# A deformable-convolution block with routed experts: output transposes one tap later, row differences two taps after their block, expert pieces in the gaps between stages

## The chip, the cores and the metric

The kernel runs on one core of a Trainium2 chip. The metric is the device time of one execution in microseconds, lower is better. The engines are TensorE (PE), VectorE (DVE), ScalarE (ACT), GpSimd (POOL) and SyncE (SP); POOL issues the indirect DMAs (gathers), SP the plain ones. Each engine works through its own list of instructions in order, and waits where an instruction's inputs or buffers are not ready.

## The reference

The input is `x`, 4 images of 256 channels and 64 x 64 positions, float32. Cut to what is computed:

```python
x = x + conv_ref(ln_c(x))          # ln_c: layer norm over channels at each position
t = to_tokens(x)                   # [4, 4096, 256]
t = t + ffn_ref(ln_t(t))           # ln_t: layer norm over each token's 256 values
return from_tokens(t)

def conv_ref(x):                   # three layers in a row
    for wo, bo, w, b in params:
        x = relu(deform_layer(x, wo, bo, w, b))
    return x

def deform_layer(x, w_off, b_off, w, b):
    om = conv3x3(x, w_off) + b_off            # 27 values at each position
    off, mask = om[:18], sigmoid(om[18:])     # (dy, dx) of 9 taps, 9 masks
    sampled = bilinear(x, base + off) * mask  # 9 samples of 256 channels each
    return einsum('bikhw,oik->bohw', sampled, w) + b

def ffn_ref(x):                    # 8 experts, the two best of each token
    probs = softmax(x @ gate_w + gate_b)
    cw = the two largest probs of each token, 0 elsewhere
    return sum over e of cw[:, e] * (gelu(x @ W1[e] + b1[e]) @ W2[e] + b2[e])
```

## The kernel before

**Stages.** The convolution work is cut into 12 stages, one for each layer and image, in the order (layer, image) = (0,0), (1,0), (0,1), (2,0), (1,1), (0,2), (2,1), (1,2), (0,3), (2,2), (1,3), (2,3); they are called stages 0 to 11. The order lets a stage's output table be finished while another image's stage runs. Only after stages 0, 10 and 11 is that not so: stages 1 and 11 gather from the table that the stage just ahead of them has filled, and after stage 11 there is no other. There `settle` runs all that is left of the side work at once.

**Blocks and taps.** A stage has 8 blocks of 512 positions, a block has 9 taps (`main_block`), and a tap has 4 samples of 128 positions. For a sample (`samples`), POOL gathers 128 rows of 4 table values for each channel (`g`, L467, 512 KB), DVE makes two interpolations (L473 and L478), ACT scales by the mask (L481). `turn` transposes samples in pairs on PE (`tp`, L496), two pairs behind the newest, and ACT copies them to `sT` (L499). `finish` multiplies a tap's `sT` by the tap's weights into `acc` (L519), and after tap 8 ACT writes the rectified rows to a window (`win`, L541).

**Tables.** Once a window's rows are there, `rows_done` starts two side generators. `store_table` makes the differences of neighbouring rows on DVE (`dd`, L272), transposes rows and differences on PE (L286), copies on ACT (`hv`, L291) and stores to the next layer's table from SP (L294). `off_block` makes the offset convolution `po` (L322) and the plan of gathers and coefficients of the next layer. In layer 2 `tokens` adds `x`, transposes, normalises, computes the gate (`lg`, L605 to L627: logits on DVE, then Exp on ACT) and the softmax and its two best (`sm`, L631, on DVE). Stages 0, 3 and 6 also prepare the tables of the next image (`pre_block`).

**Side work.** A generator put aside yields between its steps; `step(k)`, called after each tap, runs as many steps as make the list end with the block, one at least where any is left. `aside(3, ...)` says that a generator has three steps.

**Experts.** When a group of tokens is routed (`enqueue`), `begin` puts its expert steps on `tiles`, three pieces each: fetch weights and tokens (`w` L766, `zt` L778 on POOL), transposes (`ftp` L801), first product (`ph` L816), activation (`hT` L826), second product (`py` L832), bias (`y` L850 on DVE). There are five groups, images 0, 1 and 2 and the halves of image 3; `pump`, called after each tap, takes a piece each time that the group's pace allows: paces 5, 5, 2, 1.5 and 0 taps for a step. `drain` takes pieces without taps, in the last `settle` and after the last sample.

**Combine.** After a group's experts `end` queues the sums: for each 128 tokens two fetches of expert rows (`gy`, L868, on POOL, into four buffers) and two sums on DVE (`ta`, L883), at 0.5 credit, two of them to a tap. After the second of a pair the code goes on to the pair's transposes on PE (`otp`, L893), a copy on ACT (`o`, L899) and the store of the output.

**Order.** A scheduler places instructions in each engine's list. `behind()` places what is in it after the newest sample's DVE instruction (`self.last`), `later()` after the newest gather (`self.gathered`). The transposes of the sums are in neither.

Of the kernel before, what the change touches and what calls it, by code (L numbers as in the profile page):

```python
# [14 lines left out]
P = 128  # L15
# [56 lines left out]
class Group:  # L72


    def __init__(self, b, n0, n1):
        self.b, self.n0, self.n1 = b, n0, n1
        self.nm = f"{b}_{n0}"
        self.M = (n1 - n0) * TPB

        self.NF = 2 * self.M * P // FT + E - 1  # L80


        self.half = (self.NF + 1) // 2
        self.zt, self.acc, self.gy, self.py = {}, [], [], None
        self.order = [s // 2 + s % 2 * self.half for s in range(self.NF)]


class Weave:
# [3 lines left out]
    def __init__(self, ctx, tc, ins, out):  # L92
        nc = self.nc = tc.nc
        self.tc = tc
        self.ins = ins
        self.x = ins["x"].rearrange("b (c p) h w -> b p c (h w)", p=P)
        self.out_v = out.rearrange("b (c p) h w -> b p c (h w)", p=P)
        self.B = self.x.shape[0]

        def pool(name, bufs, **kw):  # L100
            return ctx.enter_context(tc.tile_pool(name=name, bufs=bufs, **kw))

        self.cst = pool("cst", 1)
        self.dram = pool("dram", 1, space=bass.MemoryType.DRAM)
        self.wkp = pool("wkp", 1)
        self.plan = pool("plan", 22)
        self.win = pool("win", 3)
        self.wt = pool("wt", 2)
        self.small = pool("small", 1)
        self.big = pool("big", 2)  # L110
        self.ffn = pool("ffn", 2)
        self.rt = pool("rt", 1)
        self.rt2 = pool("rt2", 2)
        self.gyp = pool("gyp", 4)
        self.smT = pool("smT", 2)
        self.smp = pool("smp", 8)
        self.gat = pool("gat", GB)
        self.ps = pool("ps", 3, space=bass.MemoryType.PSUM)
        self.ps1 = pool("ps1", 1, space=bass.MemoryType.PSUM)
        self.queue = []  # L120
        self.credit = 0.0
        self.side, self.plans_side = [], []
        self.last, self.gathered = None, None
        self.tiles = []
        self.tile_credit = 0.0
        self.pend, self.pairs = None, []
# [125 lines left out]
    def rows_done(self, l, b, n, wins):  # L252

        nc = self.nc
        w = wins[n]
        if n > 0:
            nc.scalar.copy(w[:, :, 0, :], wins[n - 1][:, :, RPB, :])
            nc.scalar.copy(wins[n - 1][:, :, RPB + 1, :], w[:, :, 1, :])  # L258
        self.aside(3, self.store_table(l, b, n, w))
        if n > 0:  # L260
            self.aside(6, self.off_block(l, b, n - 1, wins[n - 1]), True)
        if n == NB - 1:
            self.aside(6, self.off_block(l, b, n, w), True)

    def store_table(self, l, b, n, w):

        nc = self.nc
        nm = f"{l}_{b}_{n}"
        v = self.table(l, b).rearrange("(r c) f -> r c f", c=TC)
        dd = self.big.tile([P, CC, BLK], F32, tag="a", name=f"dd_{nm}")  # L270
        with self.behind():
            nc.vector.tensor_tensor(  # L272
                dd.rearrange("p c (r w) -> p c r w", w=W),
                w[:, :, 1 : RPB + 1, :],
                w[:, :, 0:RPB, :],
                ALU.subtract,
            )
# [32 lines left out]
    def off_block(self, l, b, n, w):  # L310
# [47 lines left out]
        yield  # L358
        with self.behind():
            nc.vector.tensor_tensor(  # L360
# [34 lines left out]
    def pre_block(self, b, n, wins, spare):  # L395
# [19 lines left out]
        rest = normalise(nc, self.small, h, h, self.eps_c, nm)  # L415
        with self.behind():
            next(rest)
        yield
        with self.behind():
            next(rest, None)  # L420
# [64 lines left out]
    def turn(self):  # L485
# [8 lines left out]
        for u in range(2):  # L494
            for c in range(CC):
                nc.tensor.transpose(  # L496
                    tp[:, c, u * P : (u + 1) * P], ss[u][:, c * P : (c + 1) * P], self.ident
# [53 lines left out]
    def tokens(self, b, n, r):  # L551
# [9 lines left out]
        yield  # L561
        with self.behind():
            nc.vector.tensor_tensor(r, r, xc, ALU.add)
# [16 lines left out]
        rest = normalise(nc, self.small, tok, z, self.eps_t, nm)  # L580
        with self.behind():
            next(rest)
        yield
        with self.behind():
            next(rest, None)
# [31 lines left out]
        yield  # L617
        with self.behind():
            nc.vector.tensor_tensor(
# [9 lines left out]
        sm = small("sm", (P, TPB))  # L629
        with self.behind():  # L630
            nc.vector.tensor_reduce(sm, lg, AX.X, ALU.add)  # L631
# [154 lines left out]
    def expert(self, grp, step):  # L786
# [20 lines left out]
        if step + 1 < grp.NF:  # L807
            with self.later():
                self.fetch(grp, step + 1)
# [31 lines left out]
    def products(self, grp):  # L841
# [6 lines left out]
        y = self.ffn.tile([P, FU, C], F32, tag="y", name=f"y_{grp.nm}_{f}")  # L848
        with self.behind():
            nc.vector.tensor_tensor(  # L850
# [7 lines left out]
    def combine_load(self, grp, n, t0):  # L858
        a = self.ffn.tile([P, 2, C], F32, tag="c", name=f"ta_{grp.nm}_{n}_{t0}")
        self.nc.sync.dma_start(a, self.t_dram[grp.b][grp.n0 + n][:, t0 : t0 + 2, :])  # L860
        grp.acc.append(a)

    def combine_fetch(self, grp, m):

        for i in range(2):
            g = self.gyp.tile([P, C], F32, tag="gy", name=f"gy_{grp.nm}_{m}_{i}")
            with self.later():
                self.nc.gpsimd.indirect_dma_start(  # L868
# [7 lines left out]
    def combine(self, grp, m):  # L876
# [3 lines left out]
        acc = grp.acc[0]  # L880
        with self.behind():
            for i in range(2):
# [3 lines left out]
                )  # L886
        if t == 0:
            return
        grp.acc.pop(0)
        tp = self.ps.tile([P, CC, 2 * P], F32, tag="tp", name=f"otp_{nm}")  # L890
        for t in range(2):
            for c in range(CC):
                nc.tensor.transpose(  # L893
                    tp[:, c, t * P : (t + 1) * P],
                    acc[:, t, c * P : (c + 1) * P],
                    self.ident,
                )
        o = self.ffn.tile([P, CC, 2 * P], F32, tag="o", name=f"o_{nm}")
        nc.scalar.copy(o, tp)  # L899
        p0 = grp.n0 * BLK + (m - 1) * P  # L900
        nc.sync.dma_start(self.out_v[grp.b, :, :, p0 : p0 + 2 * P], o)
# [19 lines left out]
    def end(self, grp):  # L921
# [64 lines left out]
    def run(self):  # L986
# [25 lines left out]
        for i, (l, b) in enumerate(self.stages):  # L1012
# [60 lines left out]
```

## Time and profile before

| | us |
|---|---|
| three runs | 7209.39, 7211.4, 7215.62 |
| median | 7211.4 |
| the profiled execution's own time | 7205.3 |
| its span in the profile | 7203.2 |

| stage | 0 | 1 | 2 | 3 | 4 | 5 | 6 | 7 | 8 | 9 | 10 | 11 |
|---|---|---|---|---|---|---|---|---|---|---|---|---|
| us from its first sample to the next stage's | 539 | 451 | 455 | 469 | 521 | 526 | 538 | 595 | 530 | 537 | 770 | 690 |

171 us lie ahead of the first sample and 413 behind the last, where the rest of the experts and the last sums run. A plain block of stages 1 and 2 takes 56.9 us. The mean clock that TensorE was granted is 0.96 of full speed. Combines fall in stages 7, 10 and 11 and behind the last sample.

How to read the lines: a group's line has the line of code, engine, operation, output and input with shapes and count, then its busy microseconds and mean nanoseconds, then the microseconds that its engine was idle just before, and what ended that. A line of waits has engine, tile and line, what ended the wait, then microseconds in all, times, longest. In the order of time a line has start, duration, engine, line, operation, and in brackets the idle time ahead of it. Matmuls are pipelined and their ends are modelled, and in the trace some of their records can be missing.

### The profile page before, as it was taken

How to read it: one execution, taken by the hardware profiler on the slowest of the kernel's cores; microseconds unless marked ns; L12 is line 12 of the kernel's file. 1: busy time of each engine (PE TensorE's matmuls, PEld its weight loads, DVE VectorE, ACT ScalarE, POOL GpSimd, SP SyncE). 2: the span in 40 equal slices, each digit the busy share in tenths (PEclk: the TensorE clock that was granted, in tenths of full speed). 3: DMA queues.
4: the chain of work that ended last, by engine and by line, in shares of the span. 5: the costliest groups of instructions: out<-in, count | busy, mean ns of one | idle time of the engine just before them, and what ended most of it. 6: DMA issues, size and time to landing. Idle time of an engine off the chain costs nothing. (4 is left out here: it accounts for less than half of the span.)

```text
span 7203.2 us, 90914 instructions
## 1 busy us (share of the span) xinstructions
PE 6450.5 (90%) x27800; PEld 3707.4 (51%) x27800; DVE 4974.0 (69%) x10828; ACT 3621.4 (50%) x7699; POOL 4291.6 (60%) x4210
## 2 busy tenths in 40 slices
PE   6899898889999999999987999999988699977987
PEld 2444444444545555556653555555555466644675
DVE  4777777778998767768876867677777465667521
ACT  4565555556764545556653455455554354544422
POOL 0654666666666656666666666666665564666543
PEclk8999999999999999999998999999999899988998
DMA  4988999989998889889998999898897787878643
GB/s 130 355 320 299 367 354 361 358 341 374 383 377 326 327 329 335 329 332 354 350 333 277 337 336 338 320 348 319 316 343 245 233 290 258 299 275 297 237 142 112
DMA packets 754764, 2224.87 MB, mean 309 GB/s; under 512 B 105880, under 2 KB 208024, under 8 KB 748520
## 3 DMA queue, kind: packets, MB, share of 16 engines
q0 software_dynamic: 549072, 1941.73, 73.3%
q1 hardware_dynamic: 205208, 277.34, 11.3%
q8 instruction: 224, 3.67, 0.2%
q14 instruction: 260, 2.13, 0.1%
HBM read 2160.68 MB, written 197.44 MB: 327 GB/s over the span
## 5 line engine op out<-in xcount | busy, mean ns | idle before, releaser
L467 POOL DMA_INDIRECT g<-tab,idx x3456 | 3516.9, 1018 | 1862.7 <-DVE s L478 687.2
L519 PE MATMUL acc<-sT,wk 128*128 128x512 f32 x6912 | 3451.5, 613 | 156.2 <-ACT sT L499 148.8
L473 DVE SCALAR_TENSOR_TENSOR g<-g,cf 128x512 f32<-128x512 f32 x3456 | 2556.5, 742 | 609.1 <-DMA g<-tab,idx 605.5
L478 DVE SCALAR_TENSOR_TENSOR s<-g,cf 128x256 f32<-128x256 f32 x3456 | 1658.6, 483 | 568.5 <-PE tp L496 270.8
L481 ACT ACTIVATE s<-s,cf 128x256 f32<-128x256 f32 x3456 | 1649.0, 509 | 675.2 <-DVE s L478 653.5
L499 ACT COPY sT<-tp 128x512 f32<-128x512 f32 x1728 | 997.6, 586 | 1592.9 <-PE tp L496 1588.0
L519 PEld LDWEIGHTS acc<-sT,wk 128*128 128x128 f32 x6912 | 1186.3, 195 | 973.8 <-issue 675.9
L496 PEld LDWEIGHTS tp<-ident,s 128*128 128x128 f32 x6912 | 886.2, 145 | 1325.8 <-ACT s L481 675.3
L496 PE MATMUL tp<-ident,s 128*128 128x128 f32 x6912 | 1258.0, 285 | 210.7 <-ACT s L481 195.9
L816 PE MATMUL ph<-fzT,w 128*128 128x256 f32 x2608 | 660.3, 387 | 34.0 <-DMA w<-in_W,wrow 16.1
L832 PE MATMUL py<-w,hT 128*128 128x256 f32 x2608 | 641.1, 387 | 30.3 <-ACT hT L826 28.3
L816 PEld LDWEIGHTS ph<-fzT,w 128*128 128x128 f32 x2608 | 476.6, 193 | 156.9 <-issue 39.3
L832 PEld LDWEIGHTS py<-w,hT 128*128 128x128 f32 x2608 | 478.9, 191 | 149.5 <-ACT hT L826 58.9
L766 POOL DMA_INDIRECT w<-in_W,wrow x163 | 169.9, 1043 | 519.5 <-issue 105.4
L826 ACT ACTIVATE hT<-ph,w 128x256 f32<-128x256 f32 x652 | 283.4, 471 | 372.2 <-PE ph L816 289.9
L778 POOL DMA_INDIRECT zt<-z,tok x326 | 335.7, 1030 | 134.6 <-issue 91.0
L868 POOL DMA_INDIRECT gy<-ys,slots x256 | 267.8, 1046 | 226.6 <-DVE ta L883 121.9
L322 PE MATMUL po<-win,wo 128*32 128x504 f32 (+1 forms) x2304 | 359.3, 600 | 14.6 <-ACT win L258 12.4
L850 DVE TENSOR_TENSOR y<-py,w 128x512 f32<-128x512 f32 x163 | 111.5, 684 | 255.8 <-PE py L832 248.2
L893 PE MATMUL otp<-ident,ta 128*128 128x128 f32 x256 | 67.8, 365 | 214.0 <-issue 145.4
L291 ACT COPY hv<-tpv 128x512 f32<-128x512 f32 x384 | 209.1, 592 | 96.7 <-PE tpv L286 72.1
L272 DVE TENSOR_TENSOR dd<-win 128x1024 f32<-128x1024 f32 x64 | 78.1, 1221 | 202.7 <-ACT win L541 202.7
(152 smaller groups left out, 3724.2 us busy)
## 6 DMA issues: line engine op xcount, KB each, us to landing
tab<-hv SPq DMA_DIRECT2D x384, 256.0 KB, 7.1
g<-tab,idx POOLq DMA_INDIRECT x3456, 6.9
ys<-y SPq DMA_DIRECT2D x163, 256.0 KB, 3.3
wk<-in_conv_w SPq DMA_DIRECT2D x108, 256.0 KB, 7.4
xc_pre<-in_x SPq DMA_DIRECT2D x32, 512.0 KB, 11.6
xr_tok<-in_x SPq DMA_DIRECT2D x32, 512.0 KB, 8.0
t<-t_tok SPq DMA_DIRECT2D x32, 512.0 KB, 5.9
ta<-t SPq DMA_DIRECT2D x64, 256.0 KB, 3.6
```

The lines of the kernel that those rows point to most:

```text
L322: nc.tensor.matmul(po[g * Q : (g + 1) * Q, :].rearrange("q (r w) -> q r w", w=W)[:, :, x0:x1], lhsT=self.wo[l][:, 3 * ky + kx, c, :], rhs= ...
L467: self.gathered = nc.gpsimd.indirect_dma_start(out=g.rearrange("p x s f -> p (x s f)"), out_offset=None, in_=self.table(*self.stages[i]), ...
L473: nc.vector.scalar_tensor_tensor(g[:, :, 0, :], g[:, :, 1, :], cf[:, j, 0:1], g[:, :, 0, :], ALU.mult, ALU.add,)
L478: self.last = nc.vector.scalar_tensor_tensor(s, g[:, 1, 0, :], cf[:, j, 1:2], g[:, 0, 0, :], ALU.mult, ALU.add)
L481: nc.scalar.activation(s, s, AF.Copy, scale=cf[:, j, 2:3])
L496: nc.tensor.transpose(tp[:, c, u * P : (u + 1) * P], ss[u][:, c * P : (c + 1) * P], self.ident)
L499: nc.scalar.copy(self.sT[:, :, t0 * P : (t0 + 2) * P], tp)
L519: nc.tensor.matmul(acc[:, o, :], lhsT=self.wk[k][:, c, o * P : (o + 1) * P], rhs=sT[:, c, :], start=(k == 0 and c == 0), stop=(k == K - 1 ...
L778: self.nc.gpsimd.indirect_dma_start(out=zt, out_offset=None, in_=grp.zd, in_offset=bass.IndirectOffsetOnAxis(ap=grp.tok[:, j : j + 1], axi ...
L816: nc.tensor.matmul(ph[:, h, :], lhsT=w1[:, o : o + P], rhs=zT[:, c, :], start=(c == 0), stop=(c == CC - 1),)
L826: nc.scalar.activation(ht[:, h, :], ph[:, h, :], AF.Gelu, bias=w1[:, k : k + 1])
L832: nc.tensor.matmul(py[:, u, :], lhsT=hT[h // 2][:, h % 2, u * P : (u + 1) * P], rhs=w2[:, h * C : (h + 1) * C], start=(h == 0), stop=(h == ...
```

## The change

- A pair's output transposes move out of `combine` into a new function `give`, which is called when the next pair's sums have been issued (one tap later), and once more at the group's end. In it the transposes are placed after the newest sample's transposes (`self.turned`). The tiles of the sums get three buffers of their tag (`bufs=3`).
- `store_table` yields once before the row differences, and is put aside for four steps.
- `settle` takes one expert piece in each of its rounds wherever `tiles` has any, and no longer only at the last stage.
- The pool of plans has 19 buffers instead of 22. `behind` and `later` become `after(self.last)` and `after(self.gathered)`, which do the same.

The diff, without the places where only `behind()` or `later()` is written anew:

```diff
@@ -81,7 +81,7 @@
 
 
         self.half = (self.NF + 1) // 2
-        self.zt, self.acc, self.gy, self.py = {}, [], [], None
+        self.zt, self.acc, self.gy, self.sums, self.py = {}, [], [], [], None
         self.order = [s // 2 + s % 2 * self.half for s in range(self.NF)]
 
 
...
@@ -103,7 +103,7 @@
         self.cst = pool("cst", 1)
         self.dram = pool("dram", 1, space=bass.MemoryType.DRAM)
         self.wkp = pool("wkp", 1)
-        self.plan = pool("plan", 22)
+        self.plan = pool("plan", 19)
         self.win = pool("win", 3)
         self.wt = pool("wt", 2)
         self.small = pool("small", 1)
...
@@ -120,7 +120,7 @@
         self.queue = []
         self.credit = 0.0
         self.side, self.plans_side = [], []
-        self.last, self.gathered = None, None
+        self.last = self.gathered = self.turned = None
         self.tiles = []
         self.tile_credit = 0.0
         self.pend, self.pairs = None, []
...
@@ -256,7 +256,7 @@
         if n > 0:
             nc.scalar.copy(w[:, :, 0, :], wins[n - 1][:, :, RPB, :])
             nc.scalar.copy(wins[n - 1][:, :, RPB + 1, :], w[:, :, 1, :])
-        self.aside(3, self.store_table(l, b, n, w))
+        self.aside(4, self.store_table(l, b, n, w))
         if n > 0:
             self.aside(6, self.off_block(l, b, n - 1, wins[n - 1]), True)
         if n == NB - 1:
...
@@ -265,10 +265,11 @@
     def store_table(self, l, b, n, w):
 
         nc = self.nc
+        yield
         nm = f"{l}_{b}_{n}"
         v = self.table(l, b).rearrange("(r c) f -> r c f", c=TC)
         dd = self.big.tile([P, CC, BLK], F32, tag="a", name=f"dd_{nm}")
-        with self.behind():
+        with self.after(self.last):
             nc.vector.tensor_tensor(
                 dd.rearrange("p c (r w) -> p c r w", w=W),
                 w[:, :, 1 : RPB + 1, :],
...
@@ -493,7 +494,7 @@
         tp = self.ps.tile([P, CC, 2 * P], F32, tag="tp", name=f"tp_{nm}_{t0}")
         for u in range(2):
             for c in range(CC):
-                nc.tensor.transpose(
+                self.turned = nc.tensor.transpose(
                     tp[:, c, u * P : (u + 1) * P], ss[u][:, c * P : (c + 1) * P], self.ident
                 )
         nc.scalar.copy(self.sT[:, :, t0 * P : (t0 + 2) * P], tp)
...
@@ -856,7 +857,7 @@
         )
 
     def combine_load(self, grp, n, t0):
-        a = self.ffn.tile([P, 2, C], F32, tag="c", name=f"ta_{grp.nm}_{n}_{t0}")
+        a = self.ffn.tile([P, 2, C], F32, tag="c", bufs=3, name=f"ta_{grp.nm}_{n}_{t0}")
         self.nc.sync.dma_start(a, self.t_dram[grp.b][grp.n0 + n][:, t0 : t0 + 2, :])
         grp.acc.append(a)
 
...
@@ -878,26 +879,34 @@
         t = m % 2
         nm = f"{grp.nm}_{m}"
         acc = grp.acc[0]
-        with self.behind():
+        with self.after(self.last):
             for i in range(2):
                 nc.vector.scalar_tensor_tensor(
                     acc[:, t, :], grp.gy.pop(0), grp.cw[:, i, m : m + 1], acc[:, t, :],
                     ALU.mult, ALU.add,
                 )
-        if t == 0:
-            return
-        grp.acc.pop(0)
+        if t == 1:
+            grp.sums.append((m - 1, grp.acc.pop(0)))
+            if len(grp.sums) > 1:
+                self.give(grp)
+
+    def give(self, grp):
+
+        nc = self.nc
+        m, acc = grp.sums.pop(0)
+        nm = f"{grp.nm}_{m}"
         tp = self.ps.tile([P, CC, 2 * P], F32, tag="tp", name=f"otp_{nm}")
-        for t in range(2):
-            for c in range(CC):
-                nc.tensor.transpose(
-                    tp[:, c, t * P : (t + 1) * P],
-                    acc[:, t, c * P : (c + 1) * P],
-                    self.ident,
-                )
+        with self.after(self.turned):
+            for t in range(2):
+                for c in range(CC):
+                    nc.tensor.transpose(
+                        tp[:, c, t * P : (t + 1) * P],
+                        acc[:, t, c * P : (c + 1) * P],
+                        self.ident,
+                    )
         o = self.ffn.tile([P, CC, 2 * P], F32, tag="o", name=f"o_{nm}")
         nc.scalar.copy(o, tp)
-        p0 = grp.n0 * BLK + (m - 1) * P
+        p0 = grp.n0 * BLK + m * P
         nc.sync.dma_start(self.out_v[grp.b, :, :, p0 : p0 + 2 * P], o)
 
 
...
@@ -928,6 +937,7 @@
             if m + 1 < grp.M:
                 put((0, lambda m=m: self.combine_fetch(grp, m + 1)))
             put((0.5, lambda m=m: self.combine(grp, m)))
+        put((0.5, lambda: self.give(grp)))
 
     def pump(self):
 
...
@@ -952,21 +962,17 @@
             for _ in range(-(-len(side) // (K - k))):
                 next(side.pop(0), None)
 
-    def behind(self):
-
-
-        return nullcontext() if self.last is None else self.tc.issue_after(self.last.ins)
-
-    def later(self):
-
-        return nullcontext() if self.gathered is None else self.tc.issue_after(self.gathered.ins)
-
-    def settle(self, last=False):
+    def after(self, newest):
+
+
+        return nullcontext() if newest is None else self.tc.issue_after(newest.ins)
+
+    def settle(self):
         while self.side or self.plans_side:
             for side in (self.side, self.plans_side):
                 if side:
                     next(side.pop(0), None)
-            if last:
+            if self.tiles:
                 self.drain(1)
 
     def drain(self, pieces):
...
@@ -1019,7 +1025,7 @@
                 while self.pairs:
                     self.turn()
                 self.finish()
-                self.settle(i + 1 == len(self.stages))
+                self.settle()
         while self.queue or self.tiles:
             self.drain(3)
 
```

More of the change, by code (lines that the diff above doesn't have):

```diff
@@ L415, in pre_block @@
         rest = normalise(nc, self.small, h, h, self.eps_c, nm)
-        with self.behind():
+        with self.after(self.last):
             next(rest)
         yield
-        with self.behind():
+        with self.after(self.last):
             next(rest, None)
@@ L561, in tokens @@
         yield
-        with self.behind():
+        with self.after(self.last):
             nc.vector.tensor_tensor(r, r, xc, ALU.add)
@@ L580, in tokens @@
         rest = normalise(nc, self.small, tok, z, self.eps_t, nm)
-        with self.behind():
+        with self.after(self.last):
             next(rest)
         yield
-        with self.behind():
+        with self.after(self.last):
             next(rest, None)
@@ L617, in tokens @@
         yield
-        with self.behind():
+        with self.after(self.last):
             nc.vector.tensor_tensor(
@@ L629, in tokens @@
         sm = small("sm", (P, TPB))
-        with self.behind():
+        with self.after(self.last):
             nc.vector.tensor_reduce(sm, lg, AX.X, ALU.add)
@@ L807, in expert @@
         if step + 1 < grp.NF:
-            with self.later():
+            with self.after(self.gathered):
                 self.fetch(grp, step + 1)
@@ L848, in products @@
         y = self.ffn.tile([P, FU, C], F32, tag="y", name=f"y_{grp.nm}_{f}")
-        with self.behind():
+        with self.after(self.last):
             nc.vector.tensor_tensor(
@@ L866, in combine_fetch @@
             g = self.gyp.tile([P, C], F32, tag="gy", name=f"gy_{grp.nm}_{m}_{i}")
-            with self.later():
+            with self.after(self.gathered):
                 self.nc.gpsimd.indirect_dma_start(
@@ L880, in combine @@
         acc = grp.acc[0]
-        with self.behind():
+        with self.after(self.last):
             for i in range(2):
```

## The prediction

> **What bounds the kernel now.** I read the page's busy shares and the 40 slices first, then the chain that ended last, the waits of DVE, PE and POOL by stage, windows of single stages, and the order of time around the three places that the change touches. The chain is no help: its largest entry is PE with 4% of the span. So each stage is read for itself.
>
> ```profile
> PE 6450.5 (90%) x27800; PEld 3707.4 (51%) x27800; DVE 4974.0 (69%) x10828; ACT 3621.4 (50%) x7699; POOL 4291.6 (60%) x4210
> ...
> L893 PE MATMUL otp<-ident,ta 128*128 128x128 f32 x256 | 67.8, 365 | 214.0 <-issue 145.4
> L272 DVE TENSOR_TENSOR dd<-win 128x1024 f32<-128x1024 f32 x64 | 78.1, 1221 | 202.7 <-ACT win L541 202.7
> ```
>
> Two idle sums stand out: PE idles 214.0 us before output transposes, DVE 202.7 us before row differences. Neither is a gain before it is known whether its engine sets the pace there.
>
> Windows of stages 1 and 3, of two combine stretches, and of the end of stage 10 (microseconds, then each engine's busy time, the clock that TensorE was granted, DMA share, GB/s):
>
> ```profile
> 710.00:1161.00 451.00, 396.62 (x1542) 182.97 (x1535) 354.36 (x692) 229.70 (x506) 295.37 (x291) 0.99 0.93 358
> 1616.00:2085.00 469.00, 433.56 (x1984) 231.92 (x1982) 420.57 (x991) 312.87 (x641) 295.05 (x289) 1.00 1.00 381
> 3743.00:3854.00 111.00, 67.62 (x204) 36.45 (x204) 56.81 (x112) 34.67 (x74) 71.50 (x70) 0.77 0.83 272
> 5594.00:5731.00 137.00, 88.66 (x372) 60.85 (x373) 63.27 (x130) 43.33 (x92) 79.81 (x81) 0.85 0.72 237
> 5985.00:6101.00 116.00, 113.09 (x542) 72.51 (x540) 57.07 (x123) 49.97 (x111) 50.50 (x51) 0.99 0.69 239
> ```
>
> Stage 1 runs on the DMA engines (share 0.93), stage 3 wholly so (1.00, DVE at 90%), the end of stage 10 on PE (113.09 of 116). In the combine stretches nothing is full: a loop of waits is at work.
>
> **Output transposes.** Order of time in stage 7, DVE, POOL and PE lines of one turn of that loop:
>
> ```profile
> 3774.61 0.75 DVE L473 SCALAR_TENSOR_TENSOR g<-g,cf 128x512 f32<-128x512 f32 x1 [7.97 <-DMA g<-tab,idx]
> 3775.87 1.67 DVE L883 SCALAR_TENSOR_TENSOR ta<-gy,cw,ta 128x256 f32<-128x256 f32 x4
> ...
> 3776.61 0.95 POOL L868 DMA_INDIRECT gy<-ys,slots  x1 [3.51 <-DVE ta L883]
> 3782.69 0.94 POOL L467 DMA_INDIRECT g<-tab,idx  x1 [0.30 <-issue]
> ...
> 3777.24 0.66 PE L893 MATMUL otp<-ident,ta 128*128 128x128 f32 x2 [8.06 <-issue]
> ...
> 3789.06 0.75 DVE L473 SCALAR_TENSOR_TENSOR g<-g,cf 128x512 f32<-128x512 f32 x1 [8.13 <-DMA g<-tab,idx]
> ```
>
> A tap lasts 3789.06 − 3774.61 = 14.45 us, against 6.3 in stage 1 (451 / 72 taps). The ring is: sums on DVE free the four gy buffers; POOL, waiting for just that (3.51 us), issues four gy fetches (6.08 us), then the sample gathers g; that of 3782.69 lands at 3789.06, 6.4 us on; two DVE operations later, at 3790.34, come the next sums. PE's 8.06 us ahead of the transposes is a wait for the same sums, beside the ring: no instruction of POOL or DVE in it waits for PE or ACT. In the instruction orders of the two kernels a pair's transposes stand, on PE, three to four samples ahead of where its sums stand on DVE; after, exactly level, for all 64 pairs. POOL's order of gy and g and DVE's order of sums do not change against each other. So the PE wait goes and the ring stays. What is late next on PE is the sample (ACT scale, after DVE). I take −3 us. The bounds are 0 and the whole wait in the three loops, 42.9 + 6.0 (stage 7), 47.7 + 14.4 (stage 10) and 54.8 (stage 11) = 166. The move lets ta loads wait for a later transpose; a third buffer pays for it, and a load lands in 3.6 us of a 14 us tap. After the last sample the final sums run on POOL's fetches, each 1.25 us apart: of the 39.0 us that PE waits for sums from stage 11 on, most lies there, behind the fetches, so −4 (0 to −39).
>
> [...]
>
> **Row differences.** Order of time at the second tap of a block of stage 1:
>
> ```profile
> 943.23 1.23 DVE L272 TENSOR_TENSOR dd<-win 128x1024 f32<-128x1024 f32 x1 [4.77 <-ACT win L541]
> ...
> 943.65 0.44 PE L496 MATMUL tp<-ident,s 128*128 128x128 f32 x2 [1.11 <-ACT s L481]
> ...
> 945.97 1.21 POOL L467 DMA_INDIRECT g<-tab,idx  x1 [6.08 <-DVE s L478]
> ```
>
> DVE stands 4.77 us for the rectified rows, which ACT finishes at 943.2. Behind it in DVE's queue stand the next samples; those hold the gather buffers; POOL stops 6.08 us; the DMA share, 1.00 to 1.04 from 905 to 940, falls to 0.70 and 0.38 in 940:950. That is (0.30 + 0.62) × 5 = 4.6 us of DMA time lost in a block of 56.9, where DMA is the bound. PE itself shows only 1.11 us of it, but its short waits in later taps (0.68 us each before acc) are DMA's pace. Moved a tap (5.9 us) later, the rows are ready, and dd has no ACT wait left in its place in stage 1. Late next are DMA (56.9 − 4.6 = 52.3) and PE (51.0 busy). I take 53: 3.9 us for each of 11 blocks whose stall is full (waits in stages 1 and 2: 28.6 + 27.3 = 55.9): −44. Bounds: 1.1 × 11 = −12, and −56. Stages 4, 5 and 8 hold 20 more such stalls (22.6 + 46.2 + 48.1 us), but there PE, with expert work to fill, is busy 499 of 526 us (2553 to 3079). Its own waits for samples, 10.4 + 14.8 + 13.4 = 39, are the ceiling; I take −15, bounds −39 and +25 for changed interleaving. The four DMA stores and transposes of each table move a tap later too, with a whole stage before the gathers that need them; SP and POOL get nothing added.
>
> The extra step that the moved work adds to the side list makes 18 where stages 3 and 6 had 17 (tokens, next image's blocks and tables). In the new order the routing's row sum follows the logits in the same tap, so on DVE it waits for the exponential behind them. In stage 3 before, logits end on DVE at 1724.52, the exponential (table load 1.28, then 0.23) at 1726.76, and samples fill the 2.2 us between. Without them: 2.2 × 16 blocks = +36 at most, 0 at least (stage 6 is PE-bound, 530.68 of 537). I take +12. Stage 9, which has this order already, shows the wait:
>
> ```profile
> DVE sm_tok L631 <- ACT lg_tok L627: 39.6, 9, 7.3
> ```
>
> [...]
>
> **Pieces in the gap.** After stage 10 the tables of image 3 must be finished before stage 11 gathers; PE has plan work and one expert step there. The new order drains about three more steps (each 8.25 us, as between 6894.65 and 6902.9 in the tail). Gain: two steps fewer in the tail, −16.5; in stage 11, eight taps fewer at pace 2 (8.67 us, from 78.0 / 9, against 6.35: −18) and three more at pace 1.5 (9.8: +10). Cost: about 6 us of expert work stands on PE ahead of the last table rows, hidden-layer activations stand ahead of the store's copy on ACT, and nine fetches of weights and tokens (1.25 us each) stand on POOL ahead of the first gather. That gather waited 37.17 us for the last table row, so the fetches hide in it unless they themselves wait. I take +9 (bounds 2 and 25). Net −15. The same gap at stage 0 has no expert work: 0 ± 3.
>
> **The sum**, on the profiled execution (7205.3; span 7203.2): −3 − 4 − 44 − 15 + 12 − 15 = −69, so 7136. The runs' median, 7211.4, lies 6 above; −69 from it is 7142. With the row differences at both ends (−56 and −39, −12 and +25) this case alone spans 7106 to 7214; with the row sum at 0 and the gap at 2 besides, it starts at 7087.
>
> **The rivals.**
> A: the PE wait was in the ring after all. Then −166 in place of −3: 6979. Against it: no DVE or POOL line of the ring waits for PE. 0.06.
> B: the dd stall was slack of which PE sees only its 1.1 us. −12 in place of −44, 0 in place of −15: 7189. For it: PE's waits sum to little; against it: the DMA share. 0.17.
> C, slower: the row sum's wait in stages 3 and 6 is as long as stage 9's longest, 7.3 us, in each of 16 blocks: +117 in place of +12, on the forecast's other terms 7247. It makes the kernel slower by over 0.2% from 69 + 12 + 14 = 95 us, or 6 us a block; with B's small return from (22 + 12 + 14) / 16 = 3 us. Against it: 39.6 / 9 = 4.4 is stage 9's mean. 0.13.
> D: no change worth measuring. B's dd, and the gap's fetches wait for buffers (+25 in place of +9) while the stage 11 taps bring nothing (8 lost): 7213. 0.12.
> The forecast has 0.52.
>
> **How the numbers follow.** About 0.2% (14 us) is what a measurement can tell from no change. Faster: the forecast, A, and 0.13 of B: 0.71. Slower: C, and a little of D: 0.15. Same: 0.14. The range leaves out A (0.06), half of C and the forecast's far tail: 7090 to 7235.
>
> **What would show it.** The windows of stages 1 and 2 should shrink from 451 and 455 to about 429 and 433 with a DMA share near 1, and DVE's wait for the rectified rows leave the waits view. The issue-ended waits of PE for output transposes should vanish, with the loop still at 14.4 us a tap: if it is shorter, the ring was misread. Stage 3 should grow by some 10 us, with a new DVE wait for the exponential; if it grows by 40, C is at work. The first gather of stage 11 should come some 9 us later after stage 10's last sample, and the tail be 16 us shorter. Stages 1 and 2 unchanged would make the prediction wrong at its largest term.

## The result and the profile after

The changed kernel takes 7214.5 us (median of 4 runs, 7208.1 to 7219.2) beside 7210.4 us for the kernel before: ratio 1.0006, 95% interval 0.9989 to 1.0023. A second measurement (e14 below) gave 1.0005, interval 0.9995 to 1.0015. So there is no change that can be told, where 69 us less were forecast.

The waits of the profile after (engine, tile and line waited for; us in total, times, longest):

```profile
PE tp L497 <- ACT s L482: 343.9, 289, 8.7
POOL gy L869 <- DVE ta L884: 137.3, 81, 7.3
PE acc L520 <- ACT sT L500: 136.5, 216, 3.2
DVE sm_tok L632 <- ACT lg_tok L628: 67.0, 25, 7.3
PE otp L902 <- DVE ta L884: 34.0, 12, 8.4
DVE dd L273 <- ACT win L542: 19.1, 3, 9.6
```

The waits that the change was aimed at did go. DVE's wait for the rectified rows fell from 202.7 to 19.1 us, and PE's issue-ended waits ahead of output transposes from 145.4 to 3.5; waits of PE for samples rose in their place from 195.9 to 343.9. Before:

```profile
PE tp L496 <- ACT s L481: 195.9, 263, 8.7
```

Almost nothing of either reached the end. The spans are 7203.2 and 7208.3; from stage to stage (first sample to first sample, and the tail behind the last):

| stage | 0 | 1 | 2 | 3 | 4 | 5 | 6 | 7 | 8 | 9 | 10 | 11 | tail |
|---|---|---|---|---|---|---|---|---|---|---|---|---|---|
| before | 539.2 | 450.9 | 454.9 | 469.4 | 520.7 | 525.9 | 537.5 | 595.1 | 529.7 | 537.1 | 769.5 | 689.9 | 412.7 |
| after | 538.8 | 448.7 | 452.5 | 467.1 | 519.2 | 528.0 | 537.4 | 613.1 | 521.8 | 537.3 | 780.1 | 690.8 | 403.2 |

Stages 1 and 2 gained 4.6 us together instead of 44. Stage 7 lost 18.0 and stage 10 lost 10.6, which nothing in the forecast accounts for. The windows of the same places as before (us, busy time and instructions of PE, PE's weight loads, DVE, ACT and POOL, granted clock, DMA share, GB/s):

```profile
709.00:1158.00 449.00, 393.40 (x1522) 183.31 (x1523) 353.21 (x687) 229.94 (x506) 306.11 (x291) 0.99 0.96 360
1610.00:2077.00 467.00, 438.50 (x1981) 235.32 (x1982) 420.38 (x991) 310.46 (x643) 308.63 (x289) 0.99 1.00 383
3749.00:3865.00 116.00, 68.51 (x199) 32.54 (x198) 56.69 (x110) 34.64 (x69) 73.23 (x71) 0.76 0.79 256
5523.00:5771.00 248.00, 184.76 (x692) 109.75 (x692) 104.42 (x219) 77.38 (x164) 144.03 (x146) 0.85 0.68 223
```

In stage 1 the DMA share went up from 0.93 to 0.96, but the block only from 56.9 to 56.7 us. The clock in a combine stretch is as low as before (0.76 and 0.77), and PE is idle as much (47 of 116 us, and 43 of 111 before), though it hardly waits for sums there: what it waits for has changed. PE's order of time in stage 7 shows the swap:

```profile
3770.44 0.69 PE L497 MATMUL tp<-ident,s 128*128 128x128 f32 x2 [5.82 <-ACT s L482]
3771.13 0.66 PE L902 MATMUL otp<-ident,ta 128*128 128x128 f32 x2
...
3783.73 0.69 PE L497 MATMUL tp<-ident,s 128*128 128x128 f32 x2 [5.47 <-ACT s L482]
```

### The profile page after: what moved, and what is told of

It is laid out like the page before. It is cut to its first block, busy times and chain, and to the rows that moved or that the text cites. A ratio compares the mean times of both kernels' runs of the same rounds, so it can differ in the third digit from the quotient of the medians.

```text
span 7208.3 us, 91034 instructions
## 1 busy us (share of the span) xinstructions
PE 6463.3 (90%) x27800; PEld 3693.0 (51%) x27800; DVE 4972.1 (69%) x10828; ACT 3617.7 (50%) x7696; POOL 4378.5 (61%) x4210
## 4 chain that ended last, share of the span: by engine, by line
PE 70%; ACT 8%; DMA 8%; DVE 6%; issue 5%; POOL 3%; SPq 0%; DVEq 0%; ACTq 0%; POOLq 0%
PE acc L520 35%; PE tp L497 10%; PE po L323 7%; PE py L833 6%; PE ph L817 6%; DMA g<-tab,idx 5%; ACT sT L500 3%; PE tpv L287 2%; DVE g L474 2%; ACT s L482 2%; POOL gy L869 2%; DVE s L479 1%; PE pm L337 1%; POOL g L468 1%; DMA tab<-hv 1%
## 5 line engine op out<-in xcount | busy, mean ns | idle before, releaser
L468 POOL DMA_INDIRECT g<-tab,idx x3456 | 3595.1, 1040 | 1759.0 <-issue 644.9
L474 DVE SCALAR_TENSOR_TENSOR g<-g,cf 128x512 f32<-128x512 f32 x3456 | 2558.3, 743 | 620.8 <-DMA g<-tab,idx 617.5
L497 PE MATMUL tp<-ident,s 128*128 128x128 f32 x6912 | 1260.9, 283 | 354.8 <-ACT s L482 343.9
L323 PE MATMUL po<-win_pre,wo 128*32 128x504 f32 (+1 forms) x1152 | 197.1, 642 | 2.5 <-ACT win_pre L258 1.5
L884 DVE SCALAR_TENSOR_TENSOR ta<-gy,cw,ta 128x256 f32<-128x256 f32 x256 | 112.9, 479 | 90.0 <-DMA gy<-ys,slots 59.1
```

Source lines behind the costliest of these rows:

```text
L323: nc.tensor.matmul(po[g * Q : (g + 1) * Q, :].rearrange("q (r w) -> q r w", w=W)[:, :, x0:x1], lhsT=self.wo[l][:, 3 * ky + kx, c, :], rhs= ...
L468: self.gathered = nc.gpsimd.indirect_dma_start(out=g.rearrange("p x s f -> p (x s f)"), out_offset=None, in_=self.table(*self.stages[i]), ...
L474: nc.vector.scalar_tensor_tensor(g[:, :, 0, :], g[:, :, 1, :], cf[:, j, 0:1], g[:, :, 0, :], ALU.mult, ALU.add,)
L497: self.turned = nc.tensor.transpose(tp[:, c, u * P : (u + 1) * P], ss[u][:, c * P : (c + 1) * P], self.ident)
```

## The experiments

Three questions were open. Where did the row differences' gain go? Which part made stages 7 and 10 longer? Did the gap pieces pay? I call the three parts rows, outputs and gap. A "combine stretch" is the time from the first to the last sum of a group, read to within 1 us; the three in question lie in stages 7, 10 and 11, and take 190, 244 and 197 us before, 203, 248 and 206 after.

**The parts alone.** e1, rows alone, from the kernel before:

```diff
-        self.aside(3, self.store_table(l, b, n, w))
+        self.aside(4, self.store_table(l, b, n, w))
...
         nc = self.nc
+        yield
```

> The kernel before with the row differences alone moved a tap later. Theory P (PE together with its short waits for ACT sets the pace of plain blocks, DVE's stall lay in PE's shadow): stages 1 and 2 fall by 2 to 3 us each as in the changed kernel, stages 7, 10 and 11 and the tail stay as before within 5 us each, the time within 10 us of before. Theory S (the row differences gain 20 us or more in stages 3 to 9, and another part of the change gives them back): the time falls by 20 to 40 us.

Measured: 7194.4 us, ratio 0.9989 (0.9980 to 0.9999). Stages 1 and 2 fell by 2.8 and 2.0 us, as under P. But stage 10 fell by 20 us, which neither theory had: its stretch took 218 us, not 244. Stage 11 fell by 7 and the tail rose by 13, so 14 of the 20 reached the end of this profile.

e2, outputs alone, is the change with the edits of rows and gap undone:

```diff
-        self.aside(4, self.store_table(l, b, n, w))
+        self.aside(3, self.store_table(l, b, n, w))
...
-        yield
...
-            if self.tiles:
+            if last:
                 self.drain(1)
```

> The kernel before with the later output transposes alone (third buffer and 19 plans with them). Theory R (the combine ring runs over POOL, DVE and the gathers; PE's wait lay beside it): 14.4 us for a tap of the loop, 0 to -5 us in all; the 18 us that stage 7 lost and the 11 of stage 10 in the changed kernel come from elsewhere or from the execution. Theory O (the later transposes lengthen the ring or what follows it): stages 7, 10 and 11 longer by 18, 5 and 10 us here too, the time 20 to 35 us up.

Measured: 7211.8 us, ratio 1.0004 (0.9995 to 1.0014); stretches of 194, 251 and 202 us. Longer by 4, 7 and 5, between the theories. Stage 7 as a whole is 9.6 us longer: outputs alone do not account for its 18.

e3, gap alone:

```diff
-            if last:
+            if self.tiles:
                 self.drain(1)
```

> The kernel before with the expert pieces in the gap behind stage 10 alone. Stages 0 to 9 have the order of before, so they show how far two executions differ. Theory G (a piece costs in the gap what it saves in the tail): stage 10 to the first samples of stage 11 +10 to +20 us, tail -14 to -17, the time within 8 us of before. Theory H (forecast): +9 and -24, the time 15 us down.

Measured: 7200.0 us, ratio 0.9996 (0.9987 to 1.0006). The last block of stage 10 took 124.5 instead of 115.6 us and the first of stage 11 92.8 instead of 76.6; the tail fell by 10.4. Its stretches, 191, 243 and 196, repeat those of before within about 1 us. The changed kernel's own repetition (e14 below) has 208, 249 and 205 beside 203, 248 and 206, so most of such a length belongs to the program, but 4 us of difference are not to be read.

e5 is rows and gap without outputs, that is the edits of e1 and e3 together:

> The changed kernel with the first part undone: output transposes with their sums as before, 22 plans; row differences and gap pieces as changed. Theory O (the later output transposes give back what the row differences gain, in the combine stretches of stages 7, 10 and 11): 10 to 15 us under before, as the row differences alone; the three stretches 198, 218 and 193 us long instead of 203, 248 and 206. Theory C (the lengths of the stretches hang on how gathers and fetches fall into POOL's list, whatever part moved them): some length between 218 and 250 in stage 10 that no part by itself foretells, the time anywhere from 12 under to 4 over before.

Measured: 7187.9 us, ratio 0.9978 (0.9969 to 0.9988), so faster by 0.22%. The stretches are 200, 221 and 202. Against the changed kernel (1.0005) the outputs cost 0.27%, some 19 us, beside rows and gap, while by themselves they cost 0.04%. What rows gain in stage 10 is what outputs take away again.

**What a combine stretch hangs on.** POOL's order of time in stage 10, first of the changed kernel:

```profile
5640.80 0.95 POOL L869 DMA_INDIRECT gy<-ys,slots  x1 [4.52 <-DVE ta L884]
...
5646.22 0.94 POOL L468 DMA_INDIRECT g<-tab,idx  x1 [0.30 <-issue]
5647.47 1.01 POOL L767 DMA_INDIRECT w<-in_W,wrow  x1 [0.30 <-issue]
5655.78 0.95 POOL L869 DMA_INDIRECT gy<-ys,slots  x1 [7.30 <-DVE ta L884]
...
5675.42 1.17 POOL L869 DMA_INDIRECT gy<-ys,slots  x1 [3.50 <-DVE pos L365]
```

then of rows alone:

```profile
5600.08 0.95 POOL L869 DMA_INDIRECT gy<-ys,slots  x1 [0.47 <-DVE ta L884]
...
5616.63 0.95 POOL L869 DMA_INDIRECT gy<-ys,slots  x1 [3.80 <-DVE ta L884]
...
5631.15 0.95 POOL L869 DMA_INDIRECT gy<-ys,slots  x1 [2.52 <-DVE ta L884]
```

In the changed kernel one gather and a weight fetch follow a tap's four gy, and POOL then stands 7.30 us; the next tap has seven gathers. From 5640.80 to 5675.42 two taps take 34.6 us. In rows alone five and three gathers lie between, and two taps take 31.1. The number of the next tap's gathers that stand ahead of a tap's gy fetches, the lead, is 3 and 0 by turns in before, e2, e3 and the changed kernel (stretches of 243 to 251 us; a few taps differ, which changes the mean by 0.1), and from the third tap on 3 and 2 in e1 and e5 (218 and 221).

My first reading was that an even order is what helps; e9 forced one:

```diff
-                self.nc.gpsimd.indirect_dma_start(                 # gy
+                self.fetched = self.nc.gpsimd.indirect_dma_start(
...
+            with self.after(self.fetched):
                 self.gathered = nc.gpsimd.indirect_dma_start(      # g
```

> The changed kernel with one order added: gathers stand on POOL behind the newest gy fetch, so that four gathers and no other number lie between the fetches of two taps, where the changed kernel has one and seven by turns in stage 10 (the kernel with the row differences alone has three and five there). Theory C (the parts move the time by how POOL's list falls in the combine stretches): the 248 us of stage 10's stretch fall to 215 to 228, the other two stay at 200 to 208, the time 15 to 30 us under the changed kernel, level with the change without its first part. Theory O (the later output transposes themselves lengthen the ring): 240 to 250 us as in the changed kernel, the time within 8 us of it.

e9 and its repetition e12 ran on two chips on which the kernel before itself takes 8274 and 8167 us, so only ratios and kernels of the same chip compare there. e9: ratio 1.0151 (1.0115 to 1.0188).

> The kernel of e9_even_gathers on another chip: gathers behind the newest gy fetch, four between the fetches of two taps everywhere. Theory C (POOL's order in the stretch makes the difference): stage 10's stretch 215 to 228 us instead of 248, the time 15 to 30 us under the changed kernel. Theory O: 240 to 250, within 8 us of it. On the other chip it was 1.5% slower than before, which neither foretold; if that is the order's doing and not the chip's, it will be slower here too, and seven gathers ahead are then worth more than an even order.

e12: 1.0129 (1.0100 to 1.0158), stretches of 266, 282 and 268 us where e13 (the version further down, with no such order forced) has 192, 224 and 193 on the same chip. The reading failed: four and four, with no gather ahead of the fetches, costs 1.3 to 1.5%. What the runs have in common is the lead, and e15 and e16 set it, one run each, with the fetches marked as in e9:

```diff
+            with self.after(self.fetched if t >= 1 else None):     # e16: t >= 2
                 self.gathered = nc.gpsimd.indirect_dma_start(
```

> The changed kernel itself, for its stretches on the chip of e15 and e16. All theories: 203, 248 and 206 us for the three combine stretches where the kernel before takes 7206, about a tenth more on a slower chip.

> The changed kernel with the second to fourth gather of a tap behind the newest gy fetch, so that at most one gather of the next tap stands ahead of a tap's fetches (three in the changed kernel's stage 7; three and none by turns in stage 10, here one and none). Theory L (the lead sets the loop): stage 7's stretch 25 to 45 us longer than in e14, stage 10's 10 to 20 longer. Theory O (the output transposes set it): all three stretches as in e14, within 5 us.

> As e15_lead_of_one, with at most two gathers ahead. Theory L: stage 7's stretch between those of e15 and e14, 10 to 25 us over e14, stage 10's 5 to 10 over. Theory O: as e14, within 5 us.

Measured on one chip: 7215.1 us (e14), 7303.7 (e15), 7277.1 (e16). Windows of the stretches of stages 7 and 10, in the order e14, e16, e15:

```profile
3702.00:3910.00 208.00, 136.99 (x477) 67.42 (x476) 103.80 (x231) 67.43 (x140) 133.42 (x125) 0.80 0.76 245
5529.00:5779.00 250.00, 184.86 (x695) 110.75 (x695) 104.83 (x222) 78.64 (x167) 142.39 (x146) 0.86 0.68 223
```

```profile
3701.00:3931.00 230.00, 142.91 (x474) 67.53 (x473) 103.50 (x227) 67.56 (x138) 125.56 (x124) 0.76 0.68 220
5550.00:5810.00 260.00, 189.06 (x689) 110.89 (x690) 104.54 (x218) 77.66 (x162) 141.12 (x146) 0.86 0.65 212
```

```profile
3695.00:3943.00 248.00, 148.51 (x475) 70.32 (x473) 106.88 (x227) 68.26 (x138) 122.94 (x126) 0.74 0.63 207
5558.00:5831.00 273.00, 199.15 (x701) 114.13 (x701) 106.69 (x220) 79.95 (x164) 140.61 (x146) 0.84 0.64 203
```

Stage 7, with a lead of 3, 2 and 1 throughout: 208, 230, 248. Stage 10, with 3, 2 and 1 in every other tap and none between: 250, 260, 273. A gather of mean lead is worth 18 to 26 us a stretch. From 3 and 0 to 3 and 2 the mean lead rises by one (by 0.75 with the first two taps of e1 and e5, which have 1 and 0), and 248 less 17 to 23 is 225 to 231, near the 218 and 221 of e1 and e5, though not all of the way. Stage 11's stretch moves in the same way, 205, 231 and 247. Theory L holds, in stage 10 by a little more than it foretold; O does not, for with the outputs' part in all three the stretches move by 40 and 23 us. The lead is not all: in stage 7 it is 3 from the sixth tap on in before, e1, e2, e5 and the changed kernel alike, and the stretch takes 190 to 208 us.

e8 tried to open the loop itself, with rows alone:

```diff
-        self.plan = pool("plan", 22)
+        self.plan = pool("plan", 19)
-        self.gyp = pool("gyp", 4)
+        self.gyp = pool("gyp", 6)
```

> The row differences alone as in e1_rows_alone, with six gy buffers instead of four (paid for with 19 plans instead of 22). Theory R (the combine ring closes over the four buffers: fetches wait for the sums just before, and the gathers behind the fetches): POOL's wait for sums nearly gone, a tap of the loop in stage 7 falls from 14.4 to POOL's own 11 us (eight issues of 1.25 and what they are stretched by), the time 60 to 130 us under before. If something else closes the ring, taps stay at 14 and the time within 15 us of e1_rows_alone.

Measured: 7184.1 us, ratio 0.9967 (0.9956 to 0.9978); stretches 198, 212 and 192 beside e1's 198, 218 and 193. POOL still waits 91.9 us for sums (e1: 93.4). The loop stays, so theory R is wrong that two more buffers open it: POOL's list now splits the fetches in twos, and the first two still stand behind the sums. The count of the lead does not carry over to six buffers: here it is 1.2 in the mean in stage 7, and the stretch is as short as e1's.

**Where the row differences went.** e7 keeps the changed kernel and only places a tap's products later on PE:

```diff
+        with self.after(self.turned):
             for o in range(CC):
                 for c in range(CC):
                     nc.tensor.matmul(
```

> The changed kernel with the products of a tap placed after the newest sample transposes, so that PE needs no copy that ACT has only just begun. Theory P: PE's 0.68 us waits before the products leave stage 1, taps of 5.9 us fall to 5.1 to 5.3, blocks of 56.7 to 53 to 54, stages 1 and 2 by 20 to 25 us each and the time by 50 to 120. Theory D: the waits move to the samples and blocks stay at 56.7.

Measured: 7123.0 us, ratio 0.9885 (0.9869 to 0.9902), 83 us less than before. PE's waits in two blocks of stage 1, in the changed kernel and then in e7, and e7's window:

```profile
PE acc L520 <- ACT sT L500: 6.7, 10, 0.7
PE tp L497 <- ACT s L482: 5.0, 12, 1.1
```

```profile
PE tp L497 <- ACT s L482: 10.9, 12, 1.0
```

```profile
831.00:941.00 110.00, 99.13 (x405) 49.47 (x406) 88.53 (x174) 58.25 (x130) 72.45 (x72) 1.00 0.96 360
```

The 0.7 us waits ahead of the products are gone and plain taps of 5.9 us became 5.4, by an order on PE alone. So those waits were PE's own: its list put a tap's products straight behind the transposes whose copy ACT had only begun. But half of the time moved, as theory D had it: PE's waits for samples rose from 5.0 to 10.9 us. Blocks fell to 55.3, not to 53 or 54, and DVE waits for the rectified rows again (96.2 us, 30 times; 2.5 us a block in this window), because late products make them late (ahead of these rows ACT waits 122.6 us in all for products in e7, 51.8 in the changed kernel).

Stages 1 and 2 fell by 13 and 9 us, not by 20 to 25. Most of the 83 us lies elsewhere: against the changed kernel's profile stages 0, 5, 7 and 9 are 32, 19, 16 and 29 us shorter, and stage 3 is 21 longer. In stage 7 the mean lead rose from 3.1 to 4.2 and the stretch fell from 203 to 182 us, which is what theory L would give; the other stages were not followed up.

e6 leaves out half of each tap's products:

```diff
-            for c in range(CC):
+            for c in range(1):
                 nc.tensor.matmul(
                     acc[:, o, :],
...
-                    stop=(k == K - 1 and c == CC - 1),
+                    stop=(k == K - 1 and c == 0),
```

> The changed kernel with half of each tap's products left out (two of four matmuls, one half of the channels). Theory P (PE and its waits for ACT set the pace of plain blocks): blocks of stage 1 fall from 56.7 to 49 to 51 us, where DVE is full. Theory D (DMA sets it): they stay above 54, with the DMA share at 1.

Measured: blocks of 52.7 to 57.4 us from the second to the seventh of stage 1, 55.7 in the mean from the third on, above P's 49 to 51 although PE is busy only 80 of 110 us:

```profile
804.00:914.00 110.00, 80.36 (x333) 37.51 (x332) 87.86 (x174) 59.03 (x130) 74.81 (x72) 0.92 0.97 365
```

Each theory is half right. PE with its waits stands at 56.7, and another limit at about 55, with the DMA share at 0.97; that DMA is that limit fits the share and was not shown by taking DMA away. e4 tried that:

```diff
-                out=g.rearrange("p x s f -> p (x s f)"),
+                out=g[:, 0].rearrange("p s f -> p (s f)"),
...
-                g[:, :, 0, :], g[:, :, 1, :], cf[:, j, 0:1], g[:, :, 0, :],
+                g[:, 1, :, :], g[:, 0, :, :], cf[:, j, 0:1], g[:, 0, :, :],
...
-                s, g[:, 1, 0, :], cf[:, j, 1:2], g[:, 0, 0, :], ALU.mult, ALU.add
+                s, g[:, 1, 0, :], cf[:, j, 1:2], g[:, 1, 1, :], ALU.mult, ALU.add
```

> The changed kernel with half of each gather left out (256 KB instead of 512; the samples are made of what is there, with as many DVE operations). Theory P: blocks of stage 1 stay at 56.7 us, within 1.5, taps at 5.9. Theory D (DMA sets the pace of plain blocks, as the forecast had it): the DMA share falls to about a half and blocks to 51 to 53 us, PE's busy time.

It is inconclusive: 7748.8 us in one run, the DMA share in stage 1 fell to 0.59, and yet blocks took 50.5 to 69.0 us, and DVE waits for gathers (2029.3 us in all, 617.5 in the changed kernel):

```profile
745.00:1244.00 499.00, 404.15 (x1530) 198.39 (x1528) 349.14 (x696) 228.02 (x508) 311.14 (x292) 0.92 0.59 174
```

More than the bytes had changed. On DVE up to six samples' first interpolations now stand in a row ahead of their second ones, where the changed kernel has one and one; the buffers of the gathers come free in clumps, and POOL has at times only 4 or 5 gathers under way where it mostly had 9 or 10. The gathers themselves were not slow: in stage 1 DVE took one up 3.8 us after its issue in the median, 13.1 us in the changed kernel. So the run shows neither that DMA is the limit at 55 us nor that it is not.

**A version that beats both.** e10, e13 and e17 are one kernel: rows and gap as changed, outputs as before, products late as in e7 (the edits of e1, e3 and e7 in the kernel before).

> The products of a tap behind the newest sample transposes (as in e7_products_late), with row differences and gap pieces as changed and the output transposes as before. If the two gains add: 7206 less 83 less another 16 to 26, near 7100. If the products' order was what stood in the way only together with the output transposes: 7120 to 7140.

> The kernel of e10_products_late_without_outputs on another chip: if the gains of the products' order (-83) and of leaving the output transposes as before (-16 to -26) add, 7095 to 7115; if they overlap, 7115 to 7140.

> Row differences and gap pieces as changed, output transposes as before, products behind the newest sample transposes (e10 and e13 again). On a chip where before takes 7206: 7095 to 7115 if the gains of e5 and e7 add, 7115 to 7140 if they overlap. On a slower chip 1.5 to 1.8% under before, as in e10 and e13.

On the two slower chips the ratios are 0.9844 (0.9805 to 0.9884) and 0.9825 (0.9788 to 0.9862). Where before takes 7209.4, it takes 7098.3 us: 0.9844 (0.9827 to 0.9860), 111 us less than before and 117 less than the changed kernel on the same chip. That lies in the range for gains of e5 and e7 that add. Its stretches are 177, 220 and 194, with a lead of 3 and 2 in stage 10. e11 moves the rows yet a tap later in it:

```diff
-        self.aside(4, self.store_table(l, b, n, w))
+        self.aside(5, self.store_table(l, b, n, w))
...
         yield
+        yield
```

> As e10_products_late_without_outputs, with the row differences yet a tap later, since with late products DVE waits for the rectified rows again (30 times, 96 us in e7_products_late). Theory P (with PE's own waits gone the stall is next): stages 1 and 2 fall by 5 to 15 us each, the time by 15 to 40 below e10. Theory D (DMA at about 55 us a block is next in stages 1 and 2): those stages stay within 5 us, the time within 15 us of e10.

Measured on the chip of e10: 8190.6 against 8152.0 us, so slower, though stages 1 and 2 fell by 7 and 3 us. Neither theory foretold a loss; I did not follow it up.

## Why the prediction was wrong

**Row differences (−44 in stages 1 and 2, measured −4.6, in e14 −5.4; −15 in stages 4, 5 and 8, measured −7.3, in e14 −3.5).** The stall went as described, and the wait is gone from the list. The step that failed is what is late next: "DMA (56.9 − 4.6 = 52.3) and PE (51.0 busy). I take 53", with PE's short waits called DMA's pace. Those ahead of the products are PE's own, by the order of its list. In a window of 57 us (869 to 926) PE works 51.1 and waits 3.4 ahead of products and 2.5 for samples; with these waits PE has no time to give back, though its work alone seems to leave 6 us. That sum by itself does not show what sets the pace; e7 does in part, for there an order on PE alone removed the waits ahead of the products and took 1.4 us off a block. The second limit was mis-sized too: in e6 and e7 blocks came down to about 55 and not to 52.3, so in these runs the term could not have been more than about 2 us a block. What holds them at 55 stays open: the DMA share is 0.96 to 0.97, and in e7 DVE's stall is back. The 4.6 us of idle DMA time was real, but idle time of an engine that is nearly full is a gain only if the next one is not as full, and PE with its waits filled the 57. Rival B had the mechanism (slack that PE does not see); the time came out as rival D's 7213, but not by D's gap: that is luck.

**Output transposes (−3 in the loops; the three stretches grew by 26 us in the whole change, 31 in e14, and by 16 with outputs alone).** The reading that PE's wait lies beside the ring was right: the wait went, and samples are late on PE in its place as said. What failed is "So the PE wait goes and the ring stays". The ring did not stay: a tap of stage 7 takes 12.6 us in the mean before and 13.5 after (the 14.45 us of the prediction is one of the longer turns). "POOL's order of gy and g and DVE's order of sums do not change against each other" does hold between the two kernels, for the lead is the same in both, 3 in stage 7, 3 and 0 in stage 10; but it is no measure of the parts. Rows and gap by themselves bring stage 10 to a lead of 3 and 2, a gain of 23 us of stretch that was not costed at all; with the outputs' part it is back at 3 and 0, and 27 us are lost (248 against 221). Why the scheduler places the fetches so was not tried. The 4 to 7 us that the outputs add to each stretch alone (e2) is not explained by the lead and stays open. The 8 us that rows add in stage 7 (e1) lie in the stretch's first five taps (70 us instead of 64), where the order on POOL differs and one gy fetch waits 9.1 us for DVE, up to plan work there (`left`, L388); before has no such wait.

**The row sum (+12, measured −2.3 in stage 3 and −0.1 in stage 6).** DVE's wait for the exponential came as forecast, 10.7 us in stage 3 and 13.4 in stage 6, but in stage 3 the wait for the logits' copy fell from 12.7 to 2.3 and the stage did not grow. Rival C is excluded. Nor are there more table loads: the traces have 164 before and 161 after, 1.283 us each.

**Gap pieces (−15, measured about −10 in e3 by stages and tail; the median's interval of −9 to +4 us does not tell it from nothing).** The gap's own price was right. From the end of stage 10's last products to the first gather of stage 11 it is 6095.3 − 6079.8 = 15.5 us before and 6107.1 − 6083.1 = 24.0 after: +8.5, forecast +9. The tail gave 9.5 us instead of 16.5, and stage 11 +0.9 instead of −8; the first block of stage 11 alone is 9 us longer (16 in e3), which the term did not have. The gather and the store of the last table row, before and then after:

```profile
6092.28 0.48 SPq L308 DMA_DIRECT2D tab<-hvl  x1
6095.26 0.96 POOL L467 DMA_INDIRECT g<-tab,idx  x1 [37.17 <-DMA tab<-hvl]
```

```profile
6103.46 0.48 SPq L309 DMA_DIRECT2D tab<-hvl  x1
6107.10 0.95 POOL L468 DMA_INDIRECT g<-tab,idx  x1 [3.73 <-issue]
```

The gather comes 3.0 us after that store is issued before and 3.6 after, so it very likely still waits for the row, though the trace names nothing; the fetches ahead of it hide in the wait, as forecast, and it is the row that comes later.

**The clock.** The granted clock in stage 7's stretch is the same, 0.77 before and 0.76 after, and PE still stands 5.82 and 5.47 us at a time there, now for samples. So what shorter waits would do to the clock was not put to the test.

## What to carry to other kernels

A stall taken from one engine pays only up to the next engine's full time, its own short waits included (here 4.6 us in stages 1 and 2 where 44 were forecast): before such waits are put down to another engine's pace, look at what stands just behind the waiting instruction's producer in its own list. Where a loop runs over an in-order queue of gathers, its period can hang on how many gathers of the next round stand ahead of the instruction that waits: here one was worth 18 to 26 us in 16 taps. A change elsewhere that reorders that queue can cost more than it gains, so the order of the queue is to be counted before and after, and for each part of a change, and not only the order of the two instructions at hand. Parts of a change need not add: measured alone, the three here are worth −0.11, +0.04 and −0.04%, all three together +0.05%, and the outputs' part costs 0.27% beside the other two.

## What was not expected of the hardware

Chips differ: the kernel before takes 7203 to 7210 us on some and 8167 and 8274 on two others. The best version moves 2224.87 MB, in e10, on a slow chip, at 272 GB/s in the mean; over e17's span of 7097.4 us on a fast one as many bytes are 313 GB/s. The granted clock is 0.915 in e10 and 0.962 in e17; what makes these chips slower was not looked into. The ratio of the best version to before was the same on the three chips on which it was measured, 0.9825 to 0.9844.
